# Four small moves in a one-core hybrid kernel: sums, a table load, a copy and the last store

## Chip, cores and metric

The kernel runs on one core of one Trainium2 chip. The metric is the device time of one execution in microseconds (us); less is better. TensorE is called PE here, its weight loads PEld, VectorE DVE, ScalarE ACT, GpSimd POOL, and SP is SyncE, whose queue issues most DMAs.

## The reference, cut to what matters

Four layers with residuals over 2 x 2048 rows of 256 fp32 features. What is computed:

```python
x = x + gated_scan(layernorm(x))    # "front": q, kv, a = rmsnorm(x) @ w_qkva; h[t] = sigmoid(a[t])*h[t-1] + kv[t]; q*h
x = x + ffn(layernorm(x))           # "front": gelu(x @ W1t + b1) @ W2t + b2, W1 and W2 made ternary
x = x + attention(layernorm(x))     # second-order linear attention, 16 heads of 64, then @ W_o
x = x + ffn(layernorm(x))           # the same ternary weights and biases once more
```

The attention keeps per head S (sums of k k^T), C (sums of q v^T) and G, and gives q (S C - G) step by step. The kernel has it in chunks of 128 rows: u comes from q, k and S, is turned into rows (uN), and M is summed from uN and v.

## The kernel before, in words

All of x stays in SBUF (`x_sb`). Rows go in chunks of 128; `blocks` are eight groups of four chunks (512 rows), the two batch rows taking turns. All matrix products are fp32, and most are made by a seven-product scheme: sums of blocks of the operands are prepared (by POOL for the right sides), seven products go through PSUM banks, and ACT and DVE copy or add each bank into the result. So every product waits for the bank that it reuses to be emptied.

Nothing is scheduled automatically: the order on PE, DVE, ACT and POOL is the order of the Python calls (`tc.manual_schedule(engines=by_hand)`), and each engine runs its own list in order. A late instruction holds up all behind it on its engine. The stages, in order of time:

- `front` (0 to about 297 us): the scan and the first ffn, interleaved. Its first part (`q_`, `a_`, `ft_`, `fw_`, ...) runs the scan of the first four blocks by `scan_part`; `ft_(0)` turns the first block for the ffn, and `fw_(0)` has POOL make its sums T1 to T4 (L512 to L515 in `ffn_rows`). `scan_rows` ends each half scan with a POOL copy of the last column (`end`, L358), which waits for DVE's scan (L356). Then a loop over the eight blocks runs `ffn_in` and `ffn_out`; in four of its rounds a generator `scan_seven` makes the next block's scan inputs in three pieces between them. Its second piece ends in three sigmoids on ACT (L418, L421, L425), its third in the copy of the last product (L430).
- In `ffn_in` a step p1 fills a bank hx (PE, L535) that ACT copies to hT (L553); p6 reuses the bank, ACT copies it again (L567), and p7 reuses it once more. Gelu (L547) follows on ACT. Sigmoid and Gelu need different function tables on ACT, and the compiler puts a table load ahead of the first use of each.
- `attention` (to about 1010 us): 32 steps s, two batch rows by 16 chunks. `Seven` makes q, k and v of two steps; its method `go(i)` runs product i, where 1, 5 and 6 end with an ACT copy (L1002, L1007, L1010) and 0 with a DVE add. `units_out(s)` turns u into blocks on DVE and sends them by DMA to DRAM, `turn_rows(s, "uN")` fetches them, and `units_end(s)` has ACT copy the fetched block, 128x1024, to uN (L1139). `update(s, "uN", "vN", "M")` multiplies it (PE, hM, L1099).
- the last ffn (to the end): seven more blocks of `ffn_in` and `ffn_out`. In `ffn_out` a `product` fills a bank of 128x256 in two halves c = 0, 1 (four matmuls each), DVE adds the bank to x (L632), and SP stores two chunks of rows (L657, L661).

Of the kernel before, what the change touches and what calls it, by code (L numbers as in the profile page):

```python
# [17 lines left out]
FP = mybir.dt.float32  # L18
# [4 lines left out]
P = 128  # L23
# [20 lines left out]
def kernel(  # L44
# [23 lines left out]
    def bank(shape, name, tag="ps"):  # L68

        ring = rings[tag]  # L70
        ring.append(ring.pop(0))
        return psum_pool.tile(shape, FP, tag=f"bank{ring[-1]}", bufs=1, name=name)
# [27 lines left out]
    w2 = early.tile([P, NF, D], FP, name="w2")  # L100
    w1_s = early.tile([P, 3, HF * P], FP, name="w1_s")
    w2_t3 = early.tile([P, 3, HF, HD], FP, name="w2_t3")

    blocks = [b * CPB + k * BC for k in range(NBLK) for b in range(B)]

# [270 lines left out]
    def scan_seven(pool, g0, A, rhs, to):  # L376

        xnT, (T1, T2, T3, T4) = rhs
        l, r = slice(0, HB), slice(HB, BT)
        Bm = {1: xnT[:, 0, l], 2: xnT[:, 1, l], 3: xnT[:, 1, r], 4: T4, 5: T1, 6: T2, 7: T3}  # L380
        to.extend(scan_room(pool, g0, e) for e in range(ND))
        a = [t[0].unsqueeze(1) for t in to]
        kq = [t[1] for t in to]
        C = {
            (t, 10 * (e + 1) + h + 1): o[e][:, :, (l, r)[h]]
            for t, o in (("a", a), ("kq", kq)) for e in range(ND) for h in range(2)
        }
        banks, begun = {}, set()

        def product(t, at, i):  # L390
            new = (t, at) not in begun
            begun.add((t, at))
            parts = (2,) if t == "a" else (1, 0)
            for j, part in enumerate(parts):
                nc.tensor.matmul(
                    banks[t, at][:, j, :], lhsT=A[i][:, part, :], rhs=Bm[i],
                    start=(new and j == 0), stop=True, skip_group_check=True,
                )

        def add(t, c, at):  # L400
            nc.vector.tensor_tensor(C[t, c], C[t, c], banks[t, at], ALU.add)

        for key in (("a", "x"), ("a", "z"), ("a", "y"), ("kq", "x"), ("kq", "y"), ("kq", "z")):
            banks[key] = bank([P, 1 if key[0] == "a" else 2, HB], "q{}{}".format(*key) + str(g0))
        for t in ("a", "kq"):
            product(t, "x", 1)
            nc.scalar.copy(C[t, 11], banks[t, "x"])
            product(t, "y", 2)
            add(t, 11, "y")
        for t in ("a", "kq"):  # L410
            product(t, "x", 6)
            nc.scalar.copy(C[t, 12], banks[t, "x"])
            product(t, "z", 5)
            nc.scalar.copy(C[t, 22], banks[t, "z"])
        yield
        product("a", "x", 7)
        add("a", 22, "x")
        nc.scalar.activation(C["a", 22], C["a", 22], AF.Sigmoid)  # L418
        product("a", "z", 3)
        add("a", 12, "z")  # L420
        nc.scalar.activation(a[0], a[0], AF.Sigmoid)  # L421
        product("kq", "x", 7)
        add("kq", 22, "x")
        product("a", "x", 4)
        nc.scalar.activation(C["a", 21], banks["a", "x"], AF.Sigmoid)  # L425
        yield
        product("kq", "z", 3)
        add("kq", 12, "z")
        product("kq", "x", 4)
        nc.scalar.copy(C["kq", 21], banks["kq", "x"])  # L430
# [174 lines left out]
    def ffn_out(sums, g0, hT, store=False, tags=("ps", "ps", "ps")):  # L605

        l, r = slice(0, HB), slice(HB, BT)
        A11, A12 = [h[:, :, l] for h in hT[:2]], [h[:, :, l] for h in hT[2:]]
        A21, A22 = [h[:, :, r] for h in hT[:2]], [h[:, :, r] for h in hT[2:]]
        cl, cr = slice(0, HD), slice(HD, D)  # L610
        lo, hi = slice(0, HF), slice(HF, NF)
        B11, B21, B22, T3 = w2[:, lo, cl], w2[:, hi, cl], w2[:, hi, cr], w2[:, lo, cr]
        T1, T2, T4 = (w2_t3[:, i] for i in range(3))
        banks = {}

        def combine(out, a, b, op):
            for h in range(2):
                nc.vector.tensor_tensor(out[h], a[h], b[h], op)  # L618

        def product(name, tag, A, Bm, i, k):  # L620
            new = name not in banks
            if new:
                banks[name] = bank([P, 2, HD], f"o{name}{g0}", tag)
            for c in range(2):
                for f in range(HF):
                    nc.tensor.matmul(  # L626
                        banks[name][:, c, :], lhsT=A[f // 2][:, f % 2, c * P : (c + 1) * P], rhs=Bm[:, f, :],
                        start=(new and c == 0 and f == 0), stop=(f == HF - 1), skip_group_check=True,
                    )
            g = g0 + 2 * (i - 1)  # L630
            xs = x_sb[:, g : g + 2, cl if k == 1 else cr]
            nc.vector.tensor_tensor(xs, xs, banks[name], ALU.add)  # L632

        def room():
            t = next(sums)
            return [t[:, :2, :], t[:, 2:, :]]

        S1, S2 = room(), room()
        combine(S1, A21, A22, ALU.add)
        combine(S2, S1, A11, ALU.subtract)  # L640
        yield
        product("x", tags[0], A11, B11, 1, 1)
        S3, S4 = room(), room()
        combine(S3, A11, A21, ALU.subtract)
        combine(S4, A12, S2, ALU.subtract)
        yield
        product("z", tags[2], S1, T1, 2, 2)
        yield
        product("x", tags[0], S2, T2, 1, 2)
        yield  # L650
        product("y", tags[1], A12, B21, 1, 1)
        yield
        product("x", tags[0], S3, T3, 2, 2)
        yield
        product("z", tags[2], S4, B22, 1, 2)
        if store:
            nc.sync.dma_start(out=rows(of, g0, 2), in_=x_sb[:, g0 : g0 + 2, :])  # L657
        yield
        product("x", tags[0], A22, T4, 2, 1)
        if store:  # L660
            nc.sync.dma_start(out=rows(of, g0 + 2, 2), in_=x_sb[:, g0 + 2 : g0 + 4, :])  # L661

    def hidden_sums(pool, g0):
# [19 lines left out]
    def front(scan_pool, ffn_pool, tern_pool, then, later):  # L683
# [92 lines left out]
        a_(3)  # L776
        rest_of = tern(w2, scales[2], 2, later=True)
        ft_(0)
        q_(4, 1)
        fw_(0)  # L780
        rest_of()
        tern(w2, scales[2], 3)
        def sums_(u):
# [134 lines left out]
    def attention(keep, pool, state, last):  # L918
# [267 lines left out]
        for s in range(NS):  # L1186
# [36 lines left out]
            if not more:  # L1223
                evict(s - 2, "oT", act if first else dve)
                last.begin(first)
                fill = last.fill
                fill(2)
                if not first:
                    units_end(s - 1)
                    units(s)  # L1230
                fill(2)
            elif first:
                if s != 2:
                    k = Seven(n + 1, "kN", "uT")
                    k.go(2)
                k.go(1)
                if s >= 2:
                    evict(s - 2, "oT")
                else:
                    units_out(s)  # L1240
                    turn_rows(s, "uN")
                k.go(0, 5)
                if s == 0:
                    k.go(6)
            else:
                if s >= 2:
                    evict(s - 2, "oT", dve)
                units_end(s - 1)
                units_out(s)
                turn_rows(s, "uN")  # L1250
                if n + 2 < CPB:
                    raw = norm_squares(pool, pair(n + 2), [xn], 2, "xraw", 1)
                if s > 1:
                    q.go(2)
                    v.go(2)
                for part in (q, v) if s > 1 else (v, q):
                    part.go(1)
                if s == NS - 3:
                    last.part()
                q.go(0, 5)  # L1260
                v.go(0, 5)
                q.go(6)
                v.go(6)
            last.part()
# [161 lines left out]
    with (  # L1426
        tc.tile_pool(name="scan", bufs=2) as scan_pool,
        tc.tile_pool(name="ffn1", bufs=2) as ffn_pool,
        tc.tile_pool(name="tern", bufs=2) as tern_pool,
        tc.manual_schedule(engines=by_hand),  # L1430
    ):

        warm = bank([P, P], "warm")
        for _ in range(12):
            nc.tensor.matmul(warm, lhsT=ones, rhs=ones, start=True, stop=True)
        table = scan_pool.tile([P, 1], FP, tag="table", name="table")
        nc.scalar.activation(table, ones[:, :1], AF.Sigmoid)
        front(
            scan_pool, ffn_pool, tern_pool, (attention_stats, attention_rows, attention_turned),
            [(lambda w=w, t=t: weights_kv(w, t)) for w, t in ((wk, wk_t), (wq, wq_t), (wv, wv_t))],  # L1440
        )
# [78 lines left out]
```

## Time and profile before

| | |
|---|---|
| median of 3 runs | 1208.22 us (1206.49 to 1210.38) |
| the profiled execution, its own time | 1209.94 us |
| its span, from first to last instruction | 1208.1 us |
| PE busy | 1196.3 us (99%) |
| DVE, ACT, POOL busy | 817.7, 618.9, 251.0 us |
| granted PE clock | 1.000 |

Busy time is the union of an engine's instructions. PE's instructions are pipelined, so one matmul overlaps the next, and a pause of PE is read from the distance of two starts rather than from the gaps between them. Lines of a timeline give the start from the beginning of the span, the length, the engine, the line, the operation, its tiles (out<-in) and its shape, how many are merged, and in brackets how long the engine was idle before and what ended that.

### The profile page before, as it was taken

How to read it: one execution, taken by the hardware profiler on the slowest of the kernel's cores; microseconds unless marked ns; L12 is line 12 of the kernel's file. 1: busy time of each engine (PE TensorE's matmuls, PEld its weight loads, DVE VectorE, ACT ScalarE, POOL GpSimd, SP SyncE). 2: the span in 40 equal slices, each digit the busy share in tenths (PEclk: the TensorE clock that was granted, in tenths of full speed). 3: DMA queues.
4: the chain of work that ended last, by engine and by line, in shares of the span. 5: the costliest groups of instructions: out<-in, count | busy, mean ns of one | idle time of the engine just before them, and what ended most of it. 6: DMA issues, size and time to landing. Idle time of an engine off the chain costs nothing.

```text
span 1208.1 us, 46645 instructions
## 1 busy us (share of the span) xinstructions
PE 1196.3 (99%) x21156; PEld 972.3 (80%) x21156; DVE 817.7 (68%) x1322; ACT 618.9 (51%) x979; POOL 251.0 (21%) x382
## 2 busy tenths in 40 slices
PE   9999999999999999999999999999999999999998
PEld 7599999999667777777777777777777889999997
DVE  7968877875567567666666766766766655677764
ACT  5356765543554554554544445455454552555442
POOL 3665235451110110110011011011001101322330
PEclk9999999999999999999999999999999999999999
DMA  9111111120244233233323323323333631212111
GB/s 331 75 62 36 36 36 35 37 71 1 89 127 130 89 119 125 91 108 134 124 83 126 128 86 125 126 90 108 125 100 100 191 100 46 71 69 72 54 53 36
DMA packets 80534, 112.99 MB, mean 94 GB/s; under 512 B 8272, under 2 KB 65488, under 8 KB 80080
## 3 DMA queue, kind: packets, MB, share of 16 engines
q1 hardware_dynamic: 77856, 106.07, 26.5%
q10 hardware_dynamic: 2448, 3.93, 1.1%
q8 instruction: 166, 2.72, 0.9%
q14 instruction: 32, 0.26, 0.1%
q0 software_dynamic: 32, 0.00, 0.0%
HBM read 58.59 MB, written 51.38 MB: 91 GB/s over the span
## 4 chain that ended last, share of the span: by engine, by line
PE 95%; DVE 1%; ACT 1%; issue 1%; DMA 1%; POOL 0%; SPq 0%; ACTq 0%; DVEq 0%; POOLq 0%
PE ox L626 10%; PE hy L1120 9%; PE hx L535 9%; PE hkN_X L988 5%; PE hqT_X L983 5%; PE hp L1042 5%; PE hvN_X L988 5%; PE oz L626 5%; PE hz L535 5%; PE pq L337 3%; PE huT L1073 3%; PE hS L1099 3%; PE huT L1059 3%; PE hoT L1059 3%; PE hM L1099 3%; PE hoT L1073 2%
## 5 line engine op out<-in xcount | busy, mean ns | idle before, releaser
L1048 DVE TENSOR_TENSOR p<-hp,mask 128x512 f32<-128x512 f32 x128 | 82.2, 683 | 82.9 <-PE hp L1042 82.9
L940 POOL TENSOR_TENSOR S<-xnT 128x128 f32<-128x128 f32 x32 | 14.7, 460 | 533.3 <-ACT xnT L281 515.6
L1120 PE MATMUL hy<-wo,oT 128*128 128x256 f32 x512 | 123.6, 385 | 0.0
L189 ACT ACTIVATE xn<-x_sb,nb,rs 128x256 f32<-128x256 f32 x124 | 65.8, 592 | 86.7 <-POOL nb L175 86.7
L1120 PEld LDWEIGHTS hy<-wo,oT 128*128 128x128 f32 x512 | 93.7, 190 | 18.9 <-issue 6.7
L547 ACT ACTIVATE hT<-hT,b_sb 128x256 f32<-128x256 f32 x192 | 85.3, 500 | 33.4 <-DVE hT L579 30.6
L1084 ACT COPY uT<-huT 128x512 f32<-128x512 f32 x32 | 18.7, 585 | 130.5 <-PE huT L1073 130.5
L1109 DVE TENSOR_TENSOR S<-S,hS 128x512 f32<-128x512 f32 x60 | 41.2, 687 | 44.8 <-PE hS L1099 41.7
L233 DVE STREAM_TRANSPOSE sqkT<-kN 128x1024 f32<-128x1024 f32 x32 | 65.9, 2059 | 1.3 <-ACT kN L1019 1.2
L1139 ACT COPY kT<-rawkT 128x1024 f32<-128x1024 f32 x32 | 66.6, 2082 | 0.0
L233 DVE STREAM_TRANSPOSE squN<-uT 128x1024 f32<-128x1024 f32 x31 | 63.6, 2051 | 4.3 <-ACT uT L1086 3.9
L1139 ACT COPY uN<-rawuN 128x1024 f32<-128x1024 f32 x31 | 64.6, 2085 | 2.4 <-DMA rawuN<-dsquN 2.0
L512 POOL TENSOR_TENSOR xT<-xnT 128x256 f32<-128x256 f32 x15 | 16.4, 1094 | 179.8 <-ACT xnT L281 118.7
L157 DVE BATCH_NORM_STATS2 st<-x_sb 128x6 f32<-128x256 f32 x128 | 51.5, 403 | 3.0 <-DMA x_sb<-in_x_dram 3.0
L1099 PEld LDWEIGHTS hS<-kN 64*64 64x64 f32 x1984 | 32.7, 134 | 23.2 <-issue 23.1
L1019 ACT COPY vN<-hvN_X 128x512 f32<-128x512 f32 x16 | 9.4, 586 | 80.1 <-PE hvN_X L988 80.1
L993 DVE TENSOR_TENSOR kN<-kN,hkN_Y 128x512 f32<-128x512 f32 x16 | 11.0, 687 | 57.7 <-ACT kN L1002 57.7
L632 DVE TENSOR_TENSOR x_sb<-x_sb,ox 128x256 f32<-128x256 f32 x64 | 26.5, 414 | 30.2 <-PE ox L626 30.2
L170 POOL TENSOR_TENSOR rs<-rs,mhalf 128x2 f32<-128x2 f32 (+1 forms) x43 | 38.4, 892 | 33.4 <-DVE rs L167 30.6
L618 DVE TENSOR_TENSOR hS<-hT 128x512 f32<-128x512 f32 x62 | 41.2, 687 | 5.6 <-ACT hT L547 5.6
L1109 DVE TENSOR_TENSOR M<-M,hM 128x512 f32<-128x512 f32 x60 | 41.1, 685 | 4.9 <-PE hM L1099 1.7
L1073 PEld LDWEIGHTS huT<-p,kN 64*64 64x64 f32 x2048 | 33.5, 134 | 13.0 <-issue 7.1
(300 smaller groups left out, 3031.9 us busy)
## 6 DMA issues: line engine op xcount, KB each, us to landing
dsqkT<-sqkT SPq DMA_DIRECT2D x32, 512.0 KB, 3.5
rawkT<-dsqkT SPq DMA_DIRECT2D x128, 128.0 KB, 2.9
dsquN<-squN SPq DMA_DIRECT2D x31, 512.0 KB, 3.6
rawuN<-dsquN SPq DMA_DIRECT2D x124, 128.0 KB, 3.2
out_dram<-x_sb SPq DMA_DIRECT2D x16, 256.0 KB, 2.2
x_sb<-in_x_dram SPq DMA_DIRECT2D x7, 512.0 KB, 8.9
dsqxn<-sqxn SPq DMA_DIRECT2D x14, 256.0 KB, 3.9
rawxn<-dsqxn SPq DMA_DIRECT2D x56, 64.0 KB, 2.5
```

Source lines behind the costliest of these rows:

```text
L233: nc.vector.transpose(to, src)
L535: nc.tensor.matmul(at[a][:, j, :], lhsT=A[:, f * P : (f + 1) * P], rhs=Bm, start=(new and j == 0), stop=True, skip_group_check=True,)
L547: nc.scalar.activation(out, out if src is None else src[:, j, :], AF.Gelu, bias=b1_sb[:, f : f + 1])
L626: nc.tensor.matmul(banks[name][:, c, :], lhsT=A[f // 2][:, f % 2, c * P : (c + 1) * P], rhs=Bm[:, f, :], start=(new and c == 0 and f == 0) ...
L988: nc.tensor.matmul(to, lhsT=self.A[i], rhs=self.B[i], start=new, stop=True, skip_group_check=True)
L1048: nc.vector.tensor_tensor(d[s][nm][:, h], banks[h], mask8, ALU.mult)
L1059: nc.tensor.matmul(banks[c][halves[h ^ c], p, :], lhsT=d[s][sums][c][halves[h], p, :], rhs=d[s]["qT"][halves[h], p, halves[c]], start=(p = ...
L1073: nc.tensor.matmul(banks[c][halves[h ^ c], p, :], lhsT=d[s][nat][halves[c], feats(h, p)], rhs=d[s][pm][halves[c], h, p, :], start=(d[s][su ...
L1099: nc.tensor.matmul(banks[c][halves[h], p, :], lhsT=d[s][left][halves[c], feats(h, p)], rhs=d[s][right][halves[c], feats(h, p)], start=True ...
L1109: nc.vector.tensor_tensor(t, prev, banks[c], ALU.add)
L1120: nc.tensor.matmul(py, lhsT=d[s]["oT"][:, p, :], rhs=wo[:, p, :], start=(p == 0), stop=(p == NPR - 1),)
L1139: act(t, d[s]["r" + nm].rearrange("p t q -> p q t"))
```

## The change

Four independent edits:

1. In the first part of `front`, `fw_(0)` (POOL's four sums for the first ffn block) is called ahead of `q_(4, 1)`, so POOL makes the sums before it copies that half scan's last column. PE's, DVE's and ACT's orders stay.
2. `scan_seven` applies Gelu to a spare 128x1 tile behind its last sigmoid. Built, the kernel has four table loads for Gelu there (one in each of the four rounds), followed by the 128x1 activation, and the four loads ahead of the first Gelu of `ffn_in` in those rounds are gone. All else on ACT keeps its order. The spare tile moves to another pool; tiles of the scan, ffn and ternary pools then lie 32 bytes lower.
3. In attention step s = 1 alone, `units_end(0)` is called behind `q.go(0, 5)` and `v.go(0, 5)`: on ACT the copy of uN moves behind four evictions (two L1002, two L1007) and stays ahead of the two L1010.
4. In the last block's last product, DVE adds each half of the bank as soon as its four matmuls are done, and SP stores each chunk of rows by its own DMA: two DVE adds of 128x128 and two DMAs of 128 KB in place of one of 128x256 and one of 256 KB. In the built kernel the first matmul of the second half waits for DVE.

```diff
+    table = early.tile([P, 1], FP, name="table")
@@ scan_seven
         nc.scalar.activation(C["a", 21], banks["a", "x"], AF.Sigmoid)
+
+        nc.scalar.activation(table, table, AF.Gelu)
         yield
@@ ffn_out
-        def product(name, tag, A, Bm, i, k):
+        def product(name, tag, A, Bm, i, k, apart=False):
...
+                if apart:
+                    nc.vector.tensor_tensor(xs[:, c], xs[:, c], banks[name][:, c], ALU.add)
+                    nc.sync.dma_start(out=rows(of, g + c, 1), in_=x_sb[:, g + c : g + c + 1, :])
+            if not apart:
+                nc.vector.tensor_tensor(xs, xs, banks[name], ALU.add)
...
-        product("x", tags[0], A22, T4, 2, 1)
-        if store:
+        final = store and g0 == blocks[-1]
+        product("x", tags[0], A22, T4, 2, 1, final)
+        if store and not final:
             nc.sync.dma_start(out=rows(of, g0 + 2, 2), in_=x_sb[:, g0 + 2 : g0 + 4, :])
@@ front
         ft_(0)
+        fw_(0)
         q_(4, 1)
-        fw_(0)
         rest_of()
@@ attention, odd steps
-                units_end(s - 1)
+                if s > 1 or not more:
+                    units_end(s - 1)
                 units_out(s)
...
                 q.go(0, 5)
                 v.go(0, 5)
+                if s == 1:
+                    units_end(s - 1)
                 q.go(6)
                 v.go(6)
@@ launch
-        table = scan_pool.tile([P, 1], FP, tag="table", name="table")
         nc.scalar.activation(table, ones[:, :1], AF.Sigmoid)
```

More of the change, by code (lines that the diff above doesn't have):

```diff
@@ L623, in product @@
                 banks[name] = bank([P, 2, HD], f"o{name}{g0}", tag)
+            g = g0 + 2 * (i - 1)
+            xs = x_sb[:, g : g + 2, cl if k == 1 else cr]
             for c in range(2):
@@ L629, in product @@
                     )
-            g = g0 + 2 * (i - 1)
-            xs = x_sb[:, g : g + 2, cl if k == 1 else cr]
-            nc.vector.tensor_tensor(xs, xs, banks[name], ALU.add)
+                if apart:
[3 more added lines that the diff above has]
+                nc.vector.tensor_tensor(xs, xs, banks[name], ALU.add)
         def room():
```

## The prediction, made before the changed kernel was run

> **What bounds the kernel now.** I read the page's busy row, then the chain of work that ended last, then the list of PE's waits, then the timeline around each wait. The first two say that PE is the bound from end to end; the third says how little it waits.
>
> ```profile
> span 1208.1 us, 46645 instructions
> ...
> PE 95%; DVE 1%; ACT 1%; issue 1%; DMA 1%; POOL 0%; SPq 0%; ACTq 0%; DVEq 0%; POOLq 0%
> ...
> PE hqT_X L983 <- ACT qT L1002: 1.0, 1, 1.0
> ...
> PE hx L535 <- ACT hT L567: 0.3, 1, 0.3
> PE hx L535 <- POOL xT L513: 0.3, 1, 0.3
> ```
>
> The last three lines (who waits <- for whom: us, times, longest) are the only places where edits 1 to 3 can win. Idle gaps understate a pause, because a matmul overlaps the next; I take the distance between starts. So the most that the three edits can bring is small, about 2 us of 1208, whatever ACT and POOL do elsewhere. No number of matmuls changes.
>
> **Edit 1, the sums.** Timeline of before:
>
> ```profile
> 58.13 0.18 POOL L358 COPY end<-kq 128x1 f32<-128x1 f32 x1 [1.16 <-DVE kq L356]
> ...
> 59.08 1.05 POOL L513 TENSOR_TENSOR xT<-xnT,xT 128x256 f32<-128x256 f32 x1
> ...
> 60.19 1.13 PE L535 MATMUL hx<-xT,w_s 128*128 128x256 f32 x4 [0.28 <-POOL xT L513]
> ```
>
> POOL idles 1.16 us until the scan is done, and the sums stand behind that. The last hy group before the PE row started at 58.88, and such a group of four takes 0.86 from start to start (57.15 to 58.01), so PE was due at 59.74 and lost 0.45. After: xnT is ready since 51.97 and POOL is free at 56.97 (58.13 - 1.16), so L512 (0.73 long at 58.28) and L513 end by 59.4 even at 1.2 us each, ahead of 59.74. What moves back is one copy of 0.18 us, needed only by the scan of block 5 around 119 us. The quarter of w2 and its sums behind it on POOL come earlier, not later. Gain 0.45, and nothing is next: the banks that the following matmuls need are emptied 0.5 us or more ahead.
>
> **Edit 2, Gelu's table.** The round where PE waits (93 to 100 us):
>
> ```profile
> 92.30 0.36 ACT L425 ACTIVATE a<-qax 128x256 f32<-128x256 f32 x1
> ...
> 93.44 0.58 ACT L430 COPY kq<-qkqx 128x512 f32<-128x512 f32 x1 [0.78 <-PE qkqx L395]
> ...
> 96.69 1.03 PE L535 MATMUL hx<-xT,w_s 128*128 128x256 f32 x4
> ...
> 96.96 1.28 ACT L547 ACT_TABLE_LOAD   x1
> ...
> 99.07 0.56 ACT L567 COPY hT<-hx 128x512 f32<-128x512 f32 x1
> ...
> 99.78 1.10 PE L535 MATMUL hx<-xT,w 128*128 128x256 f32 x4 [0.34 <-ACT hT L567]
> ```
>
> PE's previous group started at 98.42, so 99.78 is 0.50 late. After: the load starts at 92.66, where ACT was idle 0.78 us, and ends at 93.94; the 128x1 activation costs 0.20 (the same one at the start of the span took 203 ns). L430 starts at 94.14, 0.70 later. Behind it wait four norm rows (L189), two L553 and, through the rows, DVE's two stream transposes (1.1 each) and SP's DMA to DRAM and back: all about 0.7 to 0.8 later. The first L553 (94.92, 0.57 long) ends at 96.19, ahead of PE at 96.69. From 96.96 on the 1.28 us are saved: Gelu starts at 97.56 (the DVE add L561, now behind the transpose, ends at 97.4), L567 ends near 98.93 against PE's due time of 99.28. Gain 0.50. The second L561 slips to 99.04, its Gelu to 99.07 and the next L567 to 100.45, still ahead of its matmul at 101.08. The transposed block, fetched by SP, landed at 105.4 and is used by ACT at 109.5.
>
> In the other three rounds (125, 161, 196 us) PE does not wait, as its transposes L436 stand before that matmul. There I cost the edit at nothing, but the cover is thin: L430 comes 0.83 later (128.54 to 129.37), L553 ends at 131.42, and PE wants its bank at 131.79. The cover is 0.31 us, after the 0.06 that a release takes.
>
> Here a rule speaks against the edit. The Trainium skill (ScalarE: Activation LUTs, What ACT_TABLE_LOAD costs) says that a switch costs about 1283 ns for the load and 1380 ns more for a drain. The trace agrees with the first number and shows no second one: load at 96.96, Gelu at 98.26, that is 1.30 later. By the page the whole queue would slip by 1.38 more, over the cover. I take the trace, and keep the page for the rival below.
>
> **Edit 3, first u's copy.**
>
> ```profile
> 340.43 2.06 ACT L1139 COPY uN<-rawuN 128x1024 f32<-128x1024 f32 x1
> ...
> 342.39 0.58 ACT L1002 COPY vN<-hvN_X 128x512 f32<-128x512 f32 x1
> ...
> 343.52 1.16 PE L983 MATMUL hqT_X<-S,wq_t 128*128 128x128 f32 x8 [1.04 <-ACT qT L1002]
> ...
> 346.45 1.11 PE L1099 MATMUL hM<-vN,uN 64*64 64x64 f32 x64
> ```
>
> The matmul before it began at 341.45 and takes 0.86 (349.35 to 350.21), so PE was due at 342.31: 1.20 lost. After: the four evictions run at 340.43, 340.91, 341.65 and 342.50 (the last two as PE delivers), so the X bank of q is free at 341.5. The copy of uN runs from 342.99 to 345.05. Queued behind it are the two L1010, at 344.95 and 345.43, ending at 346.01; their banks are wanted at 346.29 and 347.26. uN itself is wanted by hM at 346.45 - 1.20 = 345.25. Covers of 0.2 and 0.14 us, so no new stall, or a short one. The fetch buffer that uN's copy reads is refilled by a DMA that SP issued at 347.08, when its source had landed (347.02), so SP is not held. DVE is held by its transposes until 343.4 in either order. Gain 1.20 (0.9 if the covers fail). The next wait for ACT, 0.84 at 355.98, is one product, its copy and its reader in a row, and stays.
>
> **Edit 4, the last rows.**
>
> ```profile
> 1201.67 1.95 PE L626 MATMUL ox<-w_t_back,hT 128*128 128x128 f32 x16
> ...
> 1203.65 0.42 DVE L632 TENSOR_TENSOR x_sb<-x_sb,ox 128x256 f32<-128x256 f32 x1 [1.37 <-PE ox L626]
> 1204.10 0.37 SPq L661 DMA_DIRECT2D out_dram<-x_sb  x1
> ```
>
> Sixteen passes 0.112 apart; DVE starts 0.30 after the last begins. If PE ran on, the end would gain 0.14 (an add of half size: 0.42 and 0.69 for 256 and 512 columns make 0.28 for 128). But built, the second half's first matmul waits for DVE. The Trainium skill (PSUM — Partial Sum Buffer, PSUM bank collisions raise a hardware error) says why it has to: readers and TensorE writes are to be kept apart by bank, not by address, and both halves are in one bank. So: first half's last pass 1202.45, add 1202.75 to 1203.04, PE again near 1203.09 instead of 1202.57, last pass 1203.87, add to 1204.46, DMA 1204.49: 0.39 later. The DMA has half the bytes: the 256 packets of 1 KB ran in 0.79 us on the queue (1205.04 to 1205.83), so half saves 0.39; issue and receipt stay. Sum 0.0; bounds -0.5 (no wait) and +0.5 (half a DMA is no faster).
>
> **Sum.** 0.45 + 0.50 + 1.20 + 0 = 2.15, so the span goes from 1208.1 to 1205.95. The profiled execution took 1209.94, 1.72 above the median of the runs; its "issue" pauses of PE, that no wait explains, fit (six of 0.4 to 0.9 us, 4.2 in all). Against the median: 1208.22 - 2.15 = 1206.1. That is 0.18%; about 0.3% (3.6 us) is what a measurement of this kernel can tell from no change.
>
> **Rivals.** (a) The waits come back. For: covers of 0.14 to 0.31 us. If hM waits 0.3, edit 2's round keeps half its pause and the tail costs 0.5, the gain is 1.1 and the time 1207.1. Chance 0.13. (b) Slower: a table load between sigmoid and copy drains ACT. With the page's 1.38 the first L553 of the round at 93 us ends at 97.57, 0.94 past PE's need, and 1.07 past it in three more: 4.15 lost, 1.65 still won by edits 1 and 3, time 1208.22 + 2.5 = 1210.7, more with a costly tail. It decides once ACT's delay exceeds the cover by 0.2 us per round or so. Against it: 1.30 from load to Gelu in every round, and 1.29 from load to sigmoid at 90.16. Chance 0.08. (c) The changed kernel's runs have fewer of the unexplained pauses, or the shift of the pools by 32 bytes helps: 2 us more, 1204.0. For: runs spread over 3.9 us. Against: nothing in the edits touches them. Chance 0.15. (d) My forecast: 0.64. That an edit does nothing is excluded for 1 to 3 by the built order, and part of (d) for 4.
>
> **How the numbers follow.** Forecast 1206.1, its own bounds 1205.6 to 1207.2 from the unknowns, about 1.5 more each way for medians of few runs that spread by 3.9 us. The range 1203.4 to 1209.3 takes in (a), most of (c) and leaves out most of (b). Faster by over 0.3% means under 1204.6: most of (c) and nearly a fifth of (d) and (a) by noise (1.5 us below the forecast), together 0.26. Slower by over 0.3% is over 1211.8: half of (b) and noise, 0.06. The rest, 0.68, is within.
>
> **What would show it.** In the changed profile: no PE wait on POOL xT L513 near 60, none on ACT near 99 and 343; ACT table loads at 92.7, 127.9, 163.4 and 198.9 (less 0.45 to 0.95) with L430 about 0.7 to 0.8 later against PE; hM with no wait on uN; a PE pause of about 0.5 in the last ox, and the last landing where it was after the sum of gains. Wrong: a PE wait on ACT hT L553 in the four rounds, or a hM or hvN_X wait for ACT over 0.3 near 345.

## The result: 1206.02 us, 0.23% less

The changed kernel takes 1206.02 us (median of 22 runs, 1204.98 to 1208.28). The kernel before took 1208.57 beside it (22 runs, 1206.49 to 1212.50). The ratio is 0.9977, with a 95% interval of 0.9971 to 0.9984, that is 1.9 to 3.5 us less. The forecast was 1206.1, and "within 0.3%" was its likeliest case.

From the page of the changed kernel, the span, the busy row and the chain that ended last; then its list of PE's waits (who waits <- for whom: us, times, longest):

```profile
span 1203.4 us, 46653 instructions
...
PE 1194.4 (99%) x21156; PEld 972.1 (81%) x21156; DVE 816.0 (68%) x1323; ACT 619.9 (52%) x983; POOL 252.5 (21%) x382
...
PE 98%; DVE 1%; issue 0%; DMA 0%; ACT 0%; POOL 0%; ACTq 0%; DVEq 0%; POOLq 0%
```

```profile
PE warm L1447 <- DVE ones L144: 1.0, 1, 1.0
PE huT L1082 <- issue: 1.0, 2, 0.7
PE huT L1068 <- ACT qT L1028: 0.7, 1, 0.7
PE hx L539 <- issue: 0.5, 1, 0.5
PE ox L632 <- DVE x_sb L637: 0.4, 1, 0.4
```

PE's program has the same 21156 matmul rows as before. The three waits of before that the edits aimed at (on POOL xT, on ACT hT, on ACT qT ahead of hqT_X) are gone from the list, and one wait for another engine is new: ox on DVE's add, in the last product. The wait of huT on ACT at 353 us stays, as the prediction said.

Since both kernels give PE the same matmuls in the same order, the gain can be followed row by row: the start of each matmul after, less its start before. PE's lead starts at 0.43 us (the profile of before lost that much in its first 18 us; a kernel in which no instruction moved, c_tile below, leads it by 0.40 there). Then it grows at four places and is steady between them, except for pauses that no wait explains:

| place (us of the profile before) | forecast | lead won, after | edit alone |
|---|---|---|---|
| 60 (sums) | 0.45 | 0.55, then 0.15 given back by 70 | 0.40 net |
| 99 (Gelu's table) | 0.50 | 0.57 | 0.58 |
| 128, 163, 199 (the other rounds) | 0 | 0.00 | 0.00 |
| 343 (u's copy) | 1.20 | 1.31 | 1.31 |
| last product's first matmul to the span's end | 0.00 | 0.31 | 0.30 |

The edits alone make 0.40 + 0.58 + 1.31 + 0.30 = 2.59 us. The medians differ by 2.55. The two profiled spans differ by more, 4.7 us: the 0.43 of the start, and 1.65 of pauses of PE without a releaser behind 336 us, of which the last experiments tell.

The readings that answer to those of before, all from the timeline of the changed kernel (start us, us, engine, line). Around 60 us:

```profile
57.31 0.73 POOL L517 TENSOR_TENSOR xT<-xnT,xT 128x256 f32<-128x256 f32 x1
...
58.45 1.03 PE L539 MATMUL hy<-xnT,w 128*128 128x256 f32 x4
...
59.31 1.03 PE L539 MATMUL hx<-xT,w_s 128*128 128x256 f32 x4
59.80 0.65 POOL L360 COPY end<-kq 128x1 f32<-128x1 f32 x1
```

POOL's second sum ends at 58.04, 1.27 ahead of its reader, and hx follows hy at 0.86, the spacing of groups that wait for nothing. The scan's copy now stands behind, at 59.80. Around 95 us:

```profile
91.46 0.36 ACT L427 ACTIVATE a<-qax 128x256 f32<-128x256 f32 x1
91.84 1.28 ACT L429 ACT_TABLE_LOAD   x1
93.13 0.20 ACT L429 ACTIVATE table<-table 128x1 f32<-128x1 f32 x1
93.24 0.57 ACT L434 COPY kq<-qkqx 128x512 f32<-128x512 f32 x1
...
94.70 0.57 ACT L557 COPY hT<-hx 128x512 f32<-128x512 f32 x1
...
97.44 0.57 ACT L571 COPY hT<-hx 128x512 f32<-128x512 f32 x1
...
98.44 1.03 PE L539 MATMUL hx<-xT,w 128*128 128x256 f32 x4
```

The table load starts right behind the sigmoid, the next activation follows 1.29 after the load's start, and the copy L434 0.11 after that. L571 ends at 98.01, 0.43 ahead of the matmul that used to wait for it. Around 343 us:

```profile
340.87 0.59 ACT L1016 COPY vN<-hvN_Z 128x512 f32<-128x512 f32 x1 [0.27 <-PE hvN_Z L997]
341.36 2.09 ACT L1148 COPY uN<-rawuN 128x1024 f32<-128x1024 f32 x1
341.56 1.02 PE L997 MATMUL hvN_X<-wv_t,S 128*128 128x512 f32 x2
342.52 1.16 PE L1108 MATMUL hS<-kN 64*64 64x64 f32 x64
343.33 0.60 ACT L1019 COPY qT<-hqT_X 128x512 f32<-128x512 f32 x1
343.50 1.16 PE L1108 MATMUL hM<-vN,uN 64*64 64x64 f32 x64
```

The copy of uN ends at 343.45 and hM starts at 343.50, 0.98 behind hS as in the kernel before, with no wait beside it: the cover was just enough. And the tail:

```profile
1197.30 1.06 PE L632 MATMUL ox<-w_t_back,hT 128*128 128x128 f32 x8
...
1198.39 0.29 DVE L637 TENSOR_TENSOR x_sb<-x_sb,ox 128x128 f32<-128x128 f32 x1 [0.47 <-PE ox L632]
1198.71 1.89 SPq L638 DMA_DIRECT2D out_dram<-x_sb  x2
1198.74 1.16 PE L632 MATMUL ox<-w_t_back,hT 128*128 128x128 f32 x8 [0.38 <-DVE x_sb L637]
1199.93 0.29 DVE L637 TENSOR_TENSOR x_sb<-x_sb,ox 128x128 f32<-128x128 f32 x1 [1.25 <-PE ox L632]
```

The second half of ox waits for the first half's add: PE pauses for 0.54, where 0.52 was estimated.

### The profile page after: what moved, and what is told of

Same layout as the page of the kernel before. It is cut to its first block, busy times and chain, and to the rows that moved or that the text cites. A ratio compares the mean times of both kernels' runs of the same rounds, so it can differ in the third digit from the quotient of the medians.

```text
span 1203.4 us, 46653 instructions
## 1 busy us (share of the span) xinstructions
PE 1194.4 (99%) x21156; PEld 972.1 (81%) x21156; DVE 816.0 (68%) x1323; ACT 619.9 (52%) x983; POOL 252.5 (21%) x382
## 4 chain that ended last, share of the span: by engine, by line
PE 98%; DVE 1%; issue 0%; DMA 0%; ACT 0%; POOL 0%; ACTq 0%; DVEq 0%; POOLq 0%
PE hy L1129 10%; PE ox L632 10%; PE hx L539 9%; PE hkN_X L997 5%; PE hp L1051 5%; PE hqT_X L992 5%; PE hvN_X L997 5%; PE oz L632 5%; PE hz L539 5%; PE pq L339 3%; PE huT L1082 3%; PE hS L1108 3%; PE huT L1068 3%; PE hoT L1068 3%; PE hoT L1082 3%; PE hM L1108 3%
## 5 line engine op out<-in xcount | busy, mean ns | idle before, releaser
L1002 DVE TENSOR_TENSOR kN<-kN,hkN_Y 128x512 f32<-128x512 f32 x16 | 11.0, 686 | 58.1 <-ACT kN L1011 58.1
```

## Experiments: each edit by itself

Four kernels made from the kernel before, each with one edit. "Lead" is always PE's lead over the profile of before, which takes the noise of whole runs out.

**The sums alone** (e1_sums)

```diff
         ft_(0)
-        q_(4, 1)
         fw_(0)
+        q_(4, 1)
         rest_of()
```

> Edit 1 alone. Theory (each edit wins exactly the pause of PE in front of it): PE's wait for the second sum near 60 us is gone, PE 0.45 us earlier from there to the end, the waits near 99 and 343 us stay at 0.50 and 1.20; time 0.45 less, under what the timing can show. Rival (a pause that goes comes back in a later wait): PE's lead shrinks again before 297 us.

Measured: 1208.37 against 1208.77, ratio 0.9997 (0.9989 to 1.0005). The lead goes from 0.37 to 0.92 at 59 to 62 us, falls to 0.77 by 70 and is 0.76 at 297. So 0.55 is won, and 0.15 is given back where ox waits 0.16 for ACT's hT. ACT's Gelu waits there for DVE's add L579, and that add comes only 0.75 earlier than before (65.85 instead of 66.60), while PE's matmuls come 0.92 earlier. Of the three old waits two are left in its list, and the one on POOL is gone:

```profile
PE hqT_X L983 <- ACT qT L1002: 1.0, 1, 1.0
...
PE hx L535 <- ACT hT L567: 0.3, 1, 0.3
```

**Gelu's table alone** (e2_table, with the spare tile's move)

```diff
         nc.scalar.activation(C["a", 21], banks["a", "x"], AF.Sigmoid)
+
+        nc.scalar.activation(table, table, AF.Gelu)
         yield
```

> Edit 2 alone, with the spare tile in its new pool. Theory: only the wait near 99 us goes (0.50); in the three later rounds PE's lead does not change, ACT's copy behind the table starts 0.7 to 0.8 later against PE, PE does not wait for the first eviction of hx. Rival of the prediction (a drain behind the load): load to next activation over 2 us, and PE waits of about 1 us for the eviction in three rounds, 2.5 us or more slower.

Measured: 1208.70 against 1208.77, ratio 0.9996 (0.9988 to 1.0004). The lead goes from 0.41 to 0.99 at 101.8 us and does not move in the three rounds behind it. The timing cannot see 0.58 us; the lead can.

**u's copy alone** (e3_copy)

```diff
-                units_end(s - 1)
+                if s > 1 or not more:
+                    units_end(s - 1)
                 units_out(s)
...
                 v.go(0, 5)
+                if s == 1:
+                    units_end(s - 1)
                 q.go(6)
```

> Edit 3 alone. Theory: the wait near 343 us goes, PE 1.20 earlier (to 1.35), no wait for uN at hM; time 1.2 less. Rival: the copy comes too late for hM and half or more of the 1.20 comes back there.

Measured: 1207.26 against 1208.77, ratio 0.9989 (0.9980 to 0.9997). The lead goes from 0.56 to 1.87 at 343 us, so 1.31 is won. It is the only edit that shows by itself in the times.

**The last rows alone** (e4_rows)

```diff
+                if apart:
+                    nc.vector.tensor_tensor(xs[:, c], xs[:, c], banks[name][:, c], ALU.add)
+                    nc.sync.dma_start(out=rows(of, g + c, 1), in_=x_sb[:, g + c : g + c + 1, :])
+            if not apart:
+                nc.vector.tensor_tensor(xs, xs, banks[name], ALU.add)
...
+        final = store and g0 == blocks[-1]
+        product("x", tags[0], A22, T4, 2, 1, final)
```

> Edit 4 alone. Theory: PE loses 0.54 in the last product (it waits for DVE's first add), the add is 0.14 shorter, the DMA 0.44, and the waits at the end 0.38, so the span's end comes 0.3 to 0.4 earlier. Rival: the 0.38 at the end was chance, and the edit is worth nothing or less.

Measured: 1209.13 against 1208.77, ratio 1.0002 (0.9994 to 1.0010). From the last product's first matmul to the span's end it takes 6.11 us. The kernel before and the four kernels without this edit take 6.41 to 6.43, and the others with it, where the product keeps its one bank, 6.10 to 6.12. The interval of the times holds both zero and a gain of 0.3; the traces show the gain in every kernel. Its parts, from the traces of before and after: the last DMA is issued 2.95 us after that matmul instead of 2.43 (0.52 lost); it lands after 1.72 instead of 2.16 (0.44 won, 128 KB instead of 256 KB); and the span ends 1.44 after the landing instead of 1.82 (0.38 won). The last term is in the closing waits on SP, and it is not chance: from the last landing to the end it takes 1.82 to 1.85 in the five traces without the edit, 1.44 or 1.45 in the nine with it. Before, the wait for the last store's semaphore ends at 1206.27 and the next wait only at 1206.62. After, the first half's semaphore has come at 1200.66, and the last landing (1201.96) is followed by two steps within 0.08. Why the first of these waits is followed by 0.35 us before is open.

## Experiments: the waits that could have come, and the other cases

**ACT later behind the table** (d_act_later). Five copies of a 128x128 mask onto itself delay ACT in each of the four rounds; what is computed is unchanged.

```diff
         nc.scalar.activation(table, table, AF.Gelu)
+        for _ in range(5):
+            nc.scalar.copy(mask, mask)
```

> The changed kernel with five copies of a spare 128x128 tile onto itself on ACT behind the table activation in each of the four rounds: a delay D of 1.0 to 1.4 us. Theory (the cover in front of hx is what decides, as the prediction's rival b has it): PE waits for ACT's eviction in all four rounds, D - 0.37 in the round near 95 us and D - 0.39 in the other three, 2.5 us in all for D = 1.0 and 4.1 for D = 1.4. Rival (other engines' waits cover it): under half of that.

Measured: 1211.41 against 1209.11, ratio 1.0020 (1.0013 to 1.0028). Its timeline in the second round, and its list of PE's waits:

```profile
129.47 1.60 ACT L431 COPY mask<-mask 128x128 f32<-128x128 f32 x5
...
132.44 0.57 ACT L559 COPY hT<-hx 128x512 f32<-128x512 f32 x1
...
133.16 1.10 PE L541 MATMUL hx<-xT,w_s 128*128 128x256 f32 x4 [1.04 <-ACT hT L559]
```

```profile
PE hx L541 <- ACT hT L559: 4.0, 4, 1.0
```

The copies put ACT 1.51 later. In the three later rounds PE's matmul starts 1.21 late (133.16, due at 131.95), the group behind the pause is 0.07 slower, and PE loses 1.28; in the first round it loses 1.30, and 5.1 in all. So rival (b)'s mechanism is real: the cover is 1.51 - 1.21 = 0.30, and all beyond it comes straight out of PE's time. The expectation had this mechanism with sizes that were too small: the delay is 1.51 and not 1.0 to 1.4, and for 1.51 it gives 1.12 in each of these rounds, since it lacks the slower group and takes the release too short. A drain like the one that the prediction quotes has no part in this, since the activation follows the load's start by 1.29 here too. The point of decision lies at a delay of about 0.30 us more than the edit's own. In the same timeline the eviction ends at 133.01 and PE's hx starts at 133.16: the release took 0.15, not the 0.06 that the prediction put in. It was 0.145 in all four rounds, and also at 99.78 in the trace of before, where it could have been read; the other waits for ACT, at hqT_X, huT and hM, ended 0.05 after ACT did. Why the two differ is open.

**u's copy behind the last two evictions as well** (l_copy_last)

```diff
                 q.go(0, 5)
                 v.go(0, 5)
-                if s == 1:
-                    units_end(s - 1)
                 q.go(6)
                 v.go(6)
+                if s == 1:
+                    units_end(s - 1)
```

> The changed kernel with the first copy of uN two places later, behind the two L1010 as well. Theory: the copy starts near 343.1 and ends near 345.15 in that span's time, hM was due at 343.50 and waits about 1.7 us, which takes back more than the 1.31 that edit 3 brought. Rival: hM waits for the q, k, v work and not for uN, and the place of the copy does not matter: no wait.

Measured: 1208.53 against 1209.11, ratio 0.9994 (0.9985 to 1.0002).

```profile
343.19 2.04 ACT L1148 COPY uN<-rawuN 128x1024 f32<-128x1024 f32 x1
345.29 1.16 PE L1108 MATMUL hM<-vN,uN 64*64 64x64 f32 x64 [1.53 <-ACT uN L1148]
```

Only two short evictions are moved ahead of the copy, and the lead falls from 2.87 to 1.11: 1.76 lost, of which 0.09 has come back by 353 us, so that 1.20 is left of the 1.56 that stood ahead of the edit's place. That is more than the edit brought. Of the three places tried (ahead of the evictions, behind four, behind six) the one behind four is therefore the right one, with hM's demand for uN on one side and hqT_X's demand for the bank on the other.

**The spare tile's move alone** (c_tile): before, with `table` in the other pool and no Gelu on it. It asks whether the 32 bytes matter.

```diff
+    table = early.tile([P, 1], FP, name="table")
...
-        table = scan_pool.tile([P, 1], FP, tag="table", name="table")
```

> The kernel before with the spare tile in its new pool alone: the scan, ffn and ternary tiles lie 32 bytes lower, no instruction moves. Theory: nothing, PE's starts as before up to the unexplained pauses, ratio 1.000 within 0.001. Rival (c of the prediction): part of the gain comes from the tiles' new places, ratio below 0.999.

Measured: 1209.08 against 1209.11, ratio 0.9998 (0.9990 to 1.0007). They do not: PE's lead stays at 0.40 from 20 to 330 us, and the times leave room for 1.2 us at most.

**Two banks for the last product** (t_two_banks): the kernel after, with the two halves of the last block's x products in two PSUM banks; DVE adds all of these products by halves.

```diff
+            two = name == "x" and store and g0 == blocks[-1]
...
+                if two:
+                    banks["x1"] = bank([P, 2, HD], f"ox1{g0}", "ps")
...
+                to = banks["x1" if two and c else name]
...
+                if two:
+                    nc.vector.tensor_tensor(xs[:, c], xs[:, c], to[:, c], ALU.add)
```

> The changed kernel, but in the last block the two halves of the x products lie in two PSUM banks. Theory (the half's wait is for its bank): PE's pause of 0.54 in the last product is gone, from the start of that product to the span's end 5.6 us in place of 6.10, all else as in the changed kernel; 0.5 us, too little for the timing. Rival (the wait is for DVE's add for another reason, or the time is lost elsewhere in the tail): 6.1 stays.

Measured: 1206.39 against 1209.11, ratio 0.9977 (0.9969 to 0.9985).

```profile
1198.95 1.95 PE L636 MATMUL ox<-w_t_back,hT 128*128 128x128 f32 x16
...
1200.05 0.29 DVE L641 TENSOR_TENSOR x_sb<-x_sb,ox 128x128 f32<-128x128 f32 x1 [0.47 <-PE ox L636]
```

All sixteen passes run in one piece, and DVE adds the first half while PE writes the second. From that product to the end it takes 5.49 us instead of 6.10. The 0.6 us is 0.05% and not to be seen in the times. So the pause in the tail goes with the shared bank, as the prediction took it, and it is avoidable.

## Experiments: a better kernel, and where its gain went

The longest wait for another engine that is left in the middle of the kernel is one of 0.84 us (from start to start), huT for ACT's qT at 353 us. Issuing `q.go(4)` earlier in step 1 takes it away.

**Both moves** (b_best): two banks as above, and

```diff
+            if s == 1:
+                q.go(4)
             if s >= 1:
                 inter(s - 1, "M", "oT")
                 products(s - 1, "uT", "p2")
...
-            else:
+            elif s > 1:
                 q.go(4)
```

> The changed kernel with two more edits: the last block's x products in two banks (measured alone: 6.11 to 5.49 us from the last product to the end), and in attention step s = 1 the product q.go(4) ahead of inter(0, M) and products(0), so that its copy on ACT runs beside them. Theory: the wait of 0.84 near 353 us goes too, 0.9 with the slower group behind a pause; about 1.5 us less than the changed kernel, 4.1 less than before, ratio near 0.9966. Rival: q's copy now stands behind kT's on ACT and the wait turns up at the first matmul that reads kT or q.

**The kernel after once more, on the same chip** (a_again)

> The changed kernel once more, on the chip of the one above, so that the two can be compared: ratio to before 0.997 to 0.9985, PE's waits near 60, 99 and 343 us gone as in its first profile, the unexplained pauses in other places or of other lengths.

Measured: b_best 1206.08 against 1208.48, ratio 0.9977 (0.9968 to 0.9987); a_again 1206.05, ratio 0.9978 (0.9968 to 0.9988). The second profile of the kernel after repeats the first one's leads (0.55 won and 0.14 given back, 0.58, 1.30, and 6.11 us for the tail), so they are no chance of one trace. The 1.5 us expected of b_best did not come. Its tail takes 5.49 us again, and the wait at 353 is gone, but the list of PE's waits has a new entry at its head, without a releaser, inside hp:

```profile
PE hp L1056 <- issue: 1.7, 2, 0.9
```

The pause stands at 354.39, 1.15 us long, in the middle of a group of 64x64 matmuls, the first of which had already run. Whether that was chance was asked by the next run.

**The earlier q.go(4) alone** (q_early)

> The kernel after with one move: at s = 1 q.go(4) is issued ahead of inter(0, M) and products(0), without the second bank of the last block. It takes away the 0.84 us for which huT waits for ACT's copy qT at 353.0. Theory: the pause of 1.15 us inside hp at 354 that stood in the run with both moves was chance, since pauses without a releaser differ in length from run to run at the same place; then the wait is gone, PE is about 0.9 us further ahead at 357, keeps it to the end, and the time is about 0.9 us below the kernel after (ratio to before about 0.997). Rival: the next piece of PE's instruction stream is late at that place; then a pause of about 1 us stands inside hp near 354 again, the lead of PE at 357 is within 0.3 us of the kernel after's, and the time is within 0.4 us of the kernel after's (ratio 0.9975 to 0.9980).

Measured: 1206.78 against 1208.71, ratio 0.9986 (0.9978 to 0.9994). The pause is there again, at the same matmul:

```profile
351.99 1.03 PE L1068 MATMUL huT<-qT,S 64*64 64x64 f32 x57
...
352.92 0.56 PE L1051 MATMUL hp<-qT,kT 64*64 64x64 f32 x24
354.74 0.81 PE L1051 MATMUL hp<-qT,kT 64*64 64x64 f32 x38 [1.26 <-issue]
```

At 352 PE is 1.1 us ahead of the kernel after, at 357 it is 0.40 behind, and at 359 it is 0.22 behind. The rival holds in its mechanism: the pause of about 1.5 us takes the place of the wait that was removed. It had PE within 0.3 us of the kernel after at 357 and a ratio of 0.9975 to 0.9980, and both came out a little worse.

**A shorter warm-up** (w_shift): 8 matmuls of 128x128 at the start instead of 12. The trace has two rows for each of these (24 for the 12), so PE's program is 8 matmul rows shorter ahead of everything else.

```diff
-        for _ in range(12):
+        for _ in range(8):
             nc.tensor.matmul(warm, lhsT=ones, rhs=ones, start=True, stop=True)
```

> The kernel after with 8 warm-up matmuls of 128x128 instead of 12 at the very start; nothing of the computation changes, and PE's program is 8 matmul rows (and 8 weight loads) shorter from there on. The pauses of PE without a releaser stand, over all runs so far, at rows 7979, 14240, 15390, 16412, 18712, 18823 and 19220 of PE's matmul rows counted from the program's start. Theory, a pause belongs to a place in the instruction stream (a piece of the stream that comes late): counted from the start they stay at the same numbers, so each stands 8 matmuls later in the work. Rival, a pause belongs to the work (operands, banks, addresses): each stands at the same matmul of the work, so at numbers 8 lower (7971, 16404, 18704, 19212). A third way, they belong to the time or to chance: no fixed number. The time stays within 1 us of the kernel after.

Measured: 1206.76, one run. The pauses of over 0.2 us without a releaser behind 300 us, by the number of the matmul row from the program's start (us long):

| kernel | rows |
|---|---|
| before | 2358 (.22), 7979 (.76), 14368 (.84), 16413 (.39), 17818 (.23), 18713 (.57), 18823 (.68), 19221 (.91) |
| after | 2869 (.45), 7979 (.45), 15390 (.29), 16412 (.45), 18712 (.56), 18823 (.68), 19220 (.91) |
| a_again | 2358 (.38), 7979 (.69), 14240 (.28), 15390 (.25), 16412 (.44), 18712 (.94), 18823 (.68), 19220 (.93) |
| q_early | 2741 (1.47), 2869 (.27), 4146 (.38), 7979 (.47), 15518 (.25), 16412 (.45), 17690 (.34), 18823 (.68), 19220 (1.17) |
| b_best | 2741 (1.15), 2869 (.46), 6701 (.46), 6829 (.86), 7979 (.22), 14240 (.32), 15390 (.21), 16284 (.30), 16412 (1.00), 17690 (.36), 18712 (.34), 18823 (.68), 19220 (1.18) |
| w_shift | 2869 (.44), 2996 (.84), 13090 (.28), 14240 (.32), 16540 (.20), 18815 (.69), 19220 (.92) |

The two profiles of the kernel after, the second being a_again, share six of these places (with 0.45 and 0.69 us at 7979, 0.56 and 0.94 at 18712), and three places stand in one of them alone. Two kinds of pauses can be told apart. One pause, hz to hx, moved with the work from row 18823 to 18815 and is 0.68 or 0.69 in every kernel, so it belongs to the work. Of the other six places that the expectation named, 14240 and 19220 kept their numbers, so they stand eight matmul rows later in the work; at 7979, 15390, 16412 and 18712 w_shift has no pause, neither there nor eight rows lower. 2869, which the kernel after has, kept its number too, and so did 6829 of b_best: w_shift has 0.92 us there, which the profile puts down to PE's own hoT. No pause of this kind moved by eight. They belong to places in PE's instruction stream.

These places are also spaced like pieces of it: 2741 and 2869, 6701 and 6829, 14240 and 14368, 15390 and 15518, 16284, 16412 and 16540, 17690 and 17818 lie 128 rows apart, which is 256 instructions with their weight loads. The page of the changed kernel has a queue with pieces of that size (packets, MB, share):

```profile
q8 instruction: 166, 2.72, 1.0%
```

PE's 42312 matmuls and weight loads over 166 packets are 255 for each. The traces hold each of these packets (16384 bytes) with the time at which it landed, and this ties the pauses to them. All the places lie on one grid of about 127.8 rows; let a piece be what lies between two of its points. Over all 14 traces, behind 300 us, 97 pauses of 0.2 us or more stand at the start of a piece. In each of them the last packet that had landed has the same number relative to the piece (the piece's number plus a constant), and PE goes on 1.21 to 1.62 us after that landing. The 2017 pieces that start without such a pause had their packet earlier, half of them by 2.7 us or more and only 4 by less than 1.21. So a pause of this kind is a piece of the stream that came late.

This tells where the gain of the earlier q.go(4) went. In q_early the packet of the piece at row 2741 landed at 353.44 and hp went on at 354.74; in b_best these were 353.01 and 354.39. In the kernel after it landed at 352.66 and PE, held until 353.03 by the wait for qT, reached the place at 354.38, 1.72 later: the wait for qT covered the packet. With the wait gone, the packet is the next thing that PE needs, and in both kernels it also landed later than in the kernel after. What stays open is what sets the start of a packet, and so why the same piece comes late in one run and not in the next. Neither kernel beats the kernel after by its time.

## Why the prediction was right

**The bound.** That PE sets the end, and that the three waits in its list are all that edits 1 to 3 can win, held: PE's lead changes nowhere else for a reason that the trace names.

**Edit 1: 0.45, measured 0.40.** The step "nothing is next: the banks that the following matmuls need are emptied 0.5 us or more ahead" failed: it looked at banks, and what came next was an operand. PE won 0.55 and gave 0.15 back in ox's wait for ACT's hT, since the chain from DVE's add over ACT's Gelu came forward by 0.75 only. The sum on POOL was mis-sized on the safe side (0.73 for L517, which as L513 took 1.05 before; the copy that moved back took 0.65 instead of 0.18, with nobody waiting).

**Edit 2: 0.50, measured 0.58.** The new L434 is 0.64 later against PE in this round (0.70 was worked out) and 0.78 in the second (0.83), and the three other rounds cost nothing. The 0.08 that came on top is the slower group behind the old pause. The cover in those three was put at 0.31 with a release of 0.06. In the second round of the changed kernel the eviction L557 ends at 129.94, 0.45 ahead of its reader at 130.39, which with the measured release of 0.15 leaves 0.30. The cover was right in size by luck, with terms that were off and cancelled. The choice that carried the sign was to take the trace over the rule that prices a table switch at a further 1380 ns (the Trainium skill, ScalarE: Activation LUTs, What ACT_TABLE_LOAD costs). Here nothing follows the load's 1.28 but the next activation, 1.29 after its start. With 1.38 more, the kernel would have lost about 1.15 us in each of four rounds, an estimate from the page's figure and from d_act_later (1.28 lost at a delay of 1.51).

**Edit 3: 1.20, measured 1.31.** The order on ACT came out as worked out: the four evictions start at 338.79, 339.27, 340.01 and 340.87, which with the lead of 1.64 are the predicted 340.43, 340.91, 341.65 and 342.50 within 0.01. The covers of 0.14 and 0.2 held, but barely: hM came 0.05 after the end of uN's copy (0.20 by the prediction's times), which is all that such a release takes here, and the bank of hvN_X was free 0.17 ahead of its matmul (0.28 by the prediction's times). PE came 0.11 earlier than worked out, and had that much less cover. The term that was too small is the pause itself: the group behind a pause is slower (0.99 from start to start in the kernel before, 0.89 for the same group in the kernel after), which the distance of two starts does not show. The same 0.08 to 0.11 is missing in the forecasts of edits 1 and 2.

**Edit 4: 0.0, measured 0.30.** The pause of PE (0.52 estimated, 0.54 measured) and the add (0.28, 0.29) were right, the DMA gained 0.44 instead of 0.39, and its issue came 0.52 later instead of 0.39. What the sum lacked is the 0.38 by which the closing waits got shorter; "issue and receipt stay" was true, the end behind them did not stay. The result lies within the bounds that were given (0.5 either way).

**Sum and rivals.** 2.15 was forecast and 2.59 came; all terms but the tail's were right within 0.11. That the forecast of the median was nearer (1206.1 against 1206.02) is luck: the median of before turned out 0.35 higher in more runs, which made up for most of the 0.44. Rival (a), waits that come back, shows only in the 0.15 of edit 1. Rival (b) did not happen, and d_act_later shows that its price was sized well. Of rival (c) the 32 bytes are refuted by c_tile; the pauses without a releaser gave the profile of the kernel after 1.65 us over that of before behind 336 us, and the sum of those over 0.25 us ranges from 3.4 to 7.1 over all the kernels, so they are noise larger than each of the smaller edits.

## What to carry to other kernels

When one engine is the bound and its program is unchanged, compare the starts of the same instruction in both traces: gains of 0.3 to 0.6 us stand out there that the medians of 13 runs cannot show. A wait that is removed pays only up to what the engine meets next: here the chain of two other engines took 0.15 of 0.55, and a late piece of PE's own instruction stream took all of 0.84. Before moving a long copy between two demands, work out the cover on both sides: two evictions of 0.6 us further turned 1.31 won into 0.36 lost.

## What was not expected of the hardware

- A matmul group behind a pause of PE runs slower than one in full stride: 0.97 instead of 0.86 at 60 us, 0.94 instead of 0.86 at 100, 0.99 instead of 0.89 at 343.
- The closing waits took 1.82 to 1.85 us from the last landing to the span's end in the five traces with one store at the end, and 1.44 or 1.45 in the nine in which the store was split and its first half's semaphore had come before.
- Pauses of 0.2 to 1.5 us, 3.4 to 7.1 us of them behind 300 us in one run (0.68 of that between hz and hx), stand in each kernel at some of the same places of PE's instruction stream, about 127.8 matmul rows apart or a multiple of that. The 97 of them that the 14 traces hold ended 1.21 to 1.62 us after a packet of 16384 bytes of the instruction queue had landed.
